# A two-layer convolution and attention kernel: fixed places for every operation, variance from sums made together, one PReLU term added by GpSimd, five product buffers

## The chip, the cores and the metric

The kernel runs on one core of a Trainium2 chip. The metric is the device time of one execution in microseconds (us), lower is better. Engines are called as the profile calls them: PE (TensorE, matmuls; PEld its weight loads), DVE (VectorE), ACT (ScalarE), POOL (GpSimd), SP (SyncE, which issues every DMA here). Each engine works through its own list of instructions in order; waits between engines are semaphores.

## What is computed

The input x is 16 images of 256 channels of 56 x 56 values in float32. Two residual layers follow each other; `_gn` is a group norm with 32 groups and no affine part.

```python
# layer 0
xq = sign(_gn(x) + bias)
out = 0
for i, d in enumerate((1, 3, 5)):                 # three dilations
    y = conv3x3(xq, binary_weight(w[i]), dilation=d, groups=4)
    y = y + cb[i] - move1[i]
    y = where(y >= 0, y, alpha[i] * y)            # PReLU
    out = out + y + move2[i]
mean, var = out.mean(channels), out.var(channels)
x = x + (out - mean) * rsqrt(var + 1e-5) * gamma + beta
# layer 1
q, k, v = split(qkv_w @ _gn(x) + qkv_b)           # 8 heads of 8 channels each
k, v = unfold3x3(k) + dwconv(k) + ..., unfold3x3(v) + dwconv(v) + ...
attn = softmax((q * k).sum(channel), over the 9 neighbours)
x = x + proj_w @ (attn * v).sum(neighbours) + proj_b
```

## The kernel before

Two half images lie one above the other on the 128 partitions (64 channels of a group each), so that a matmul works on quarters of the array. An image is cut into two *units* (u = 0, 1), each of 7 rows in each quarter of the image: a full-size operation covers 128 partitions x 784 values (2 x 392, two PSUM banks). PSUM is a ring of four such double banks (`banks`, kind "ps").

For an image b, the stages are:

- `stats`, `norm0`, `sign` (lines 420 to 457): load the four channel groups, sum and sum of squares on ACT with its accumulator (L424), the group norm's shift, the sign into a padded bf16 tile `sgn` (L449), then halo copies by DMA.
- `conv{u}` (lines 489 to 540): for each of 4 groups and 3 dilations, 36 matmuls of `sgn` and `wconv` into one double bank (L499). The PReLU of it is written as alpha times the value plus (1 - alpha) times Relu. Into the tile `ct` go: for the first dilation a scaled copy on ACT (L518), for the other two a multiply-add on DVE that reads PSUM and `ct` (L525); then Relu in place on ACT (L531), and for all three a second multiply-add on DVE (L537), after which the bank is free.
- `mean{u}`, `var{u}`, `root{u}`, `scale{u}` (lines 576 to 654): the layer norm over channels. All four `ct` are summed over channels by PE (L548), ACT copies the sum (L588), PE spreads it to all partitions (L566), DVE subtracts it from each `ct` (L595; `mv2`, the constant part of the PReLUs, is added here too), ACT squares (L602), PE sums the squares into a bank of its own. Small operations on ACT and DVE (L612 to L617) make the inverse root with one Newton step, PE spreads it, DVE multiplies (L624), POOL adds the result to the residual `xt` (L638), ACT takes the squares for the next group norm (L645).
- `fold` (lines 657 to 721): the second group norm is folded into the QKV weights `wf` (POOL, L667) and a bias.
- `qkv{u}` (lines 723 to 765): 48 matmuls per unit (L729), evicted by ACT into `qt`, `kt`, `vt`.
- `prod{u}`, `term{u}`, `soft{u}` (lines 776 to 844): for each of 9 neighbours a product of q and the shifted k, `p` (L785, three buffers), which PE sums into scores of four heads (L807; the bias term, first, waits for the first three products); a 32 x 32 transpose, the softmax on DVE, ACT and POOL, and a transpose back into `at`.
- `value{u}`, `proj{u}` (lines 846 to 926): for each of 10 terms PE spreads the weights (L857), DVE multiplies by the shifted v (L869), and the terms are summed into the first one (L883); PE projects (L903), DVE adds to `xt` (L914), and the unit is stored by four DMAs (L924).

All operations are first recorded in a `Plan` and then issued in an order that the plan makes (lines 113 to 232). Each recorded operation has its engine, a planned cost and a priority: twice the image number plus a number that `ORDER` gives for its stage and its index in the stage. `Plan.emit` keeps a planned clock for every engine and every buffer, and takes again and again the ready operation that can start first, with the priority as the second key, so that the order of the engines' lists comes from planned costs. `either` (lines 357 to 361) records an operation that POOL or DVE may do: POOL, unless DVE would be done earlier by the margin `LEAN` (by `LAST` in the last image). By the trace this put all adds L638, all products L785 but 12 of the last image, and all value adds L883 but 5 of the last image on POOL. The lists of the engines repeat from image to image in the middle of the program, and mix the convolutions of one image with the attention of the image before it.

Of the kernel before, what the change touches and what calls it, by code (L numbers as in the profile page):

```python
# [2 lines left out]

# [11 lines left out]
P = 128  # L15
# [4 lines left out]
PADC = 5  # L20
# [25 lines left out]


# [11 lines left out]
class Buf:  # L59


    def __init__(self, kind):
        self.kind, self.left, self.tile, self.end = kind, 0, None, 0.0
# [5 lines left out]
class Op:  # L69
    def __init__(self, engines, prio, emit, bufs, port, late):  # L70
        self.engines, self.prio, self.emit = engines, prio, emit
        self.bufs, self.port, self.late = bufs, port, late
        self.after, self.wait, self.ready = [], 0, 0.0

ORDER = {
    "first": (-3.81,),
    "second": (88.59,),
    "start": (-2.38, 18.89, -7.71, 3.29),  # L80
    "weights": (-4.65, -9.01, 0.64, 24.68, 23.33, 21),
    "stats": (10.49, 30.86, 22.58, 94.91),
    "norm0": (32.82,),
    "sign": (19.48, 99.46, -6.27, -5.4),
    "conv0": (-1.69, 4.96, 26.11, 0.66, 0.85, 19.36, -4.07, -1.86, 4.93, -11.22, -8.26, 19.59),
    "conv1": (-5.78, -8.78, 98.87, 0.22, 0.26, 6.89, -8.83, 30.63, 33.62, 1.84, 19.38, 25.39),
    "load0": (90.92,),
    "load1": (8.24,),
    "mean0": (-9.77,),
    "mean1": (20.13,),  # L90
    "var0": (-12.01, -8.88, 19.47, -0.22),
    "var1": (-14.66, 26.56, 89.22, -12.67),
    "root0": (23.78,),
    "root1": (-9.89,),
    "scale0": (100.7, 21.53, 3.58, 99.01),
    "scale1": (-10.73, -4.27, -0.4, 21.4),
    "fold": (-8.77,),
    "qkv0": (-0.15, -11.55, 19.01),
    "qkv1": (10.85, 1.84, 96.23),
    "prod0": (28.81, -0.84, -7.11, -6.13, -10.3, 7.62, -0.09, -4.95, 20.71),  # L100
    "prod1": (27.44, 23.38, -3.2, 99.25, 31.01, -10.92, -1.88, -1.61, -3.25),
    "term0": (19.37, 27.66, 25.15, 17.81, -9.38, 9.45, -1.68, 20.87, -1.36, 21.48),
    "term1": (24.14, 22.52, 28.6, 3.33, 8.91, 2.55, 1.92, 35.5, 4.7, 21.73),
    "soft0": (-4.91,),
    "soft1": (7.25,),
    "value0": (8.34, -0.46, -5.88, 1.95, 0.4, 8.91, 0.58, 26.08, -5.98, 34.72),
# [6 lines left out]
class Plan:  # L113

    HOP = 0.1
    LEAN = 26.94
    LAST = -11.31
    AHEAD = 0.13

# [41 lines left out]
    def emit(self):  # L167
# [4 lines left out]
        while ready:  # L172
            short, best = set(), {}
            for x in ready:
# [15 lines left out]
                if held:  # L190
                    continue
# [1041 lines left out]
```

## Time and profile before

| | us |
|---|---|
| median of three runs | 2156.07 |
| lowest, highest | 2154.64, 2160.12 |
| the profiled execution, as timed | 2157.43 |
| its span, first to last instruction | 2154.9 |
| DVE L537, second multiply-add, x384, mean of one | 1.027 |
| DVE L525, multiply-add of two dilations, x256, mean of one | 1.024 |
| ACT L518, scaled copy of the first dilation, x128, mean of one | 0.910 |
| DVE L595, subtraction of the mean, x128, mean of one | 1.023 |
| DVE L869, product with v, x288, mean of one | 0.969 |
| POOL L785, products, x276, mean of one | 1.726 |
| POOL L883, value adds, x251, mean of one | 1.906 |
| POOL L638, residual adds, x128, mean of one | 1.860 |
| mean granted clock of PE, as a share | 0.948 |

The profile gives for each group of instructions their busy time and what ended the idle time of the engine before them. The busy shares are means over the whole span; what a change in one stage is worth is read from windows of that stage and from the timeline, where an idle time of an engine stands in brackets together with the instruction that ended it. Neighbouring instructions on DVE overlap a little, so that their distance from start to start is somewhat less than the duration of one.

### The profile page before, as it was taken

What the parts mean: (1) busy time and instruction counts of PE and PEld (TensorE: products, weight loads), DVE (VectorE), ACT (ScalarE), POOL (GpSimd) and SP (SyncE); (2) the same over time, 40 slices, a digit from 0 to 9 for tenths busy, and PEclk for the clock granted to TensorE, in tenths of its full rate; (3) what the DMA queues carried; (4) which work ended last, traced back from release to release, by engine and by line L of the source; (5) the groups of instructions that cost most, each with busy time, mean ns of one, the idle gap of its engine ahead of it and who ended that gap; (6) DMA issues with size and microseconds to landing.
All of it is one profiled execution on the core that took longest, in us unless ns stands there. A gap on an engine that the chain in (4) does not pass through costs nothing.

```text
span 2154.9 us, 70853 instructions
## 1 busy us (share of the span) xinstructions
PE 1823.2 (85%) x31770; PEld 889.5 (41%) x31770; DVE 1697.7 (79%) x2327; ACT 1189.6 (55%) x1581; POOL 1276.5 (59%) x762
## 2 busy tenths in 40 slices
PE   6679898888989889898988989898898989879684
PEld 5444353434435343443534344353434435434231
DVE  7676969789696977969698796968879696986856
ACT  8675556565565756556575655647565565533220
POOL 2116657585675748557574865747486574746743
PEclk9889999999999999999999999999999999989896
DMA  8742534644453454445445444644444454041212
GB/s 208 165 92 67 123 79 111 130 95 91 110 130 83 111 121 97 93 104 133 91 111 117 100 94 95 138 94 111 108 102 101 95 133 100 7 100 23 61 31 60
DMA packets 102416, 216.26 MB, mean 100 GB/s; under 512 B 10720, under 2 KB 84832, under 8 KB 102112
## 3 DMA queue, kind: packets, MB, share of 16 engines
q1 hardware_dynamic: 102112, 211.74, 44.5%
q8 instruction: 248, 4.06, 0.8%
q14 instruction: 56, 0.46, 0.1%
HBM read 154.91 MB, written 51.38 MB: 96 GB/s over the span
## 4 chain that ended last, share of the span: by engine, by line
PE 42%; DVE 32%; POOL 10%; ACT 7%; issue 7%; DMA 2%; SPq 0%; POOLq 0%; DVEq 0%; ACTq 0%
PE banks L499 13%; PE banks L729 10%; PE banks L807 8%; POOL m L883 6%; DVE m L869 6%; DVE ct L537 6%; PE banks L857 5%; DVE ct L525 5%; DVE xt L914 4%; ACT banks L531 3%; DVE ct L595 3%; POOL xt L638 2%; PE banks L566 2%; PE banks L903 2%; DVE et L821 1%
## 5 line engine op out<-in xcount | busy, mean ns | idle before, releaser
L499 PE MATMUL banks<-sgn,wconv 64*64 64x392 bf16 x13824 | 680.2, 340 | 78.9 <-DVE m L869 32.1
L785 POOL TENSOR_TENSOR p<-qt,kt 128x784 f32<-128x784 f32 x276 | 467.0, 1726 | 326.2 <-ACT kt L762 179.3
L883 POOL TENSOR_TENSOR m<-m 128x784 f32<-128x784 f32 x251 | 478.3, 1906 | 248.1 <-DVE m L869 232.8
L499 PEld LDWEIGHTS <-wconv 64*64 64x64 bf16 x13824 | 438.6, 107 | 373.4 <-issue 217.4
L531 ACT ACTIVATE banks<-banks,cbi,csc 128x784 f32<-128x784 f32 x384 | 370.2, 973 | 203.2 <-DVE ct L525 192.4
L537 DVE SCALAR_TENSOR_TENSOR ct<-banks,oalpha,ct 128x784 f32<-128x784 f32 x384 | 389.4, 1027 | 98.4 <-ACT banks L531 89.3
L525 DVE SCALAR_TENSOR_TENSOR ct<-banks,asc,ct 128x784 f32<-128x784 f32 x256 | 262.0, 1024 | 186.9 <-PE banks L499 180.7
L857 PE MATMUL banks<-at,wv 64*32 64x392 f32 x5120 | 300.0, 533 | 61.3 <-DVE m L869 44.2
L638 POOL TENSOR_TENSOR xt<-xt,ct 128x784 f32<-128x784 f32 x128 | 237.2, 1860 | 190.4 <-DVE ct L624 189.6
L869 DVE TENSOR_TENSOR m<-banks,vt 128x784 f32<-128x784 f32 x288 | 278.2, 969 | 54.8 <-PE banks L857 48.7
L807 PE MATMUL banks<-p,wk 32*64 32x392 f32 x4608 | 245.4, 517 | 38.6 <-POOL p L785 38.2
L729 PE MATMUL banks<-xt,wf 64*64 64x392 f32 x3072 | 269.0, 496 | 2.8 <-POOL wf L667 2.8
L424 ACT ACTIVATE junk<-xh 128x1568 bf16<-128x1568 f32 x128 | 193.2, 1509 | 103.2 <-DMA xh<-in_x 101.4
L645 ACT ACTIVATE junk<-xt,pr 128x784 bf16<-128x784 f32 x128 | 121.2, 947 | 106.4 <-POOL xt L638 105.2
L602 ACT ACTIVATE sq<-ct 128x784 f32<-128x784 f32 x128 | 109.4, 857 | 125.2 <-DVE ct L595 102.5
L518 ACT ACTIVATE ct<-banks,asc 128x784 f32<-128x784 f32 x128 | 116.4, 910 | 98.8 <-PE banks L499 87.5
L729 PEld LDWEIGHTS banks<-xt,wf 64*64 64x64 f32 x3072 | 116.0, 134 | 129.2 <-issue 104.4
L857 PEld LDWEIGHTS banks<-at,wv 64*32 64x32 f32 x5120 | 63.3, 108 | 220.6 <-DVE m L869 110.9
L807 PEld LDWEIGHTS banks<-p,wk 32*64 32x64 f32 x4608 | 80.3, 133 | 161.1 <-POOL p L785 83.0
L903 PE MATMUL banks<-m,wp 64*64 64x392 f32 x1024 | 122.3, 584 | 26.1 <-DVE m L891 21.8
L595 DVE SCALAR_TENSOR_TENSOR ct<-ct,mv,banks 128x784 f32<-128x784 f32 x128 | 125.4, 1023 | 17.4 <-PE banks L566 17.4
L914 DVE SCALAR_TENSOR_TENSOR xt<-banks,prb,xt 128x784 f32<-128x784 f32 x128 | 128.1, 1028 | 10.4 <-PE banks L903 9.7
(102 smaller groups left out, 1518.8 us busy)
## 6 DMA issues: line engine op xcount, KB each, us to landing
xh<-in_x SPq DMA_DIRECT2D x248, 392.0 KB, 5.6
xt<-in_x SPq DMA_DIRECT2D x128, 392.0 KB, 7.1
out<-xt SPq DMA_DIRECT2D x128, 392.0 KB, 5.8
sgn<-sgn SPq DMA_DIRECT2D x128, 41.2 KB, 4.7
p<-in_w SPq DMA_DIRECT2D x12, 144.0 KB, 5.9
wq<-in_wqkv SPq DMA_DIRECT2D x1, 384.0 KB, 6.1
cst<-in_consts SPq DMA_DIRECT2D x1, 336.0 KB, 2.9
wk<-in_wk_a SPq DMA_DIRECT2D x1, 320.0 KB, 5.8
```

The costliest lines, as they stand in the source:

```text
L499: nc.tensor.matmul(out=ps[q * GC : (q + 1) * GC, h, 0:SN], lhsT=wconv[h * GC : (h + 1) * GC, g, d, tap, :], rhs=sgn[g][h * GC : (h + 1) * ...
L525: lambda: nc.vector.scalar_tensor_tensor(ct.tile, n(), asc[:, g, s], ct.tile, ALU.mult, ALU.add),
L531: lambda: nc.scalar.activation(n(), n(), AF.Relu, bias=cbi[:, g, s], scale=csc[:, g, s]),
L537: lambda: nc.vector.scalar_tensor_tensor(ct.tile, n(), oalpha[:, g, s], ct.tile, ALU.mult, ALU.add),
L638: lambda e, g=g: e.tensor_tensor(xt[:, g], xt[:, g], ct[g].tile, ALU.add),
L729: nc.tensor.matmul(out=ps[h * D : (h + 1) * D, q, 0:SN], lhsT=wf[q * GC : (q + 1) * GC, g, j, :], rhs=xt[q * GC : (q + 1) * GC, g, h, :], ...
L785: e.tensor_tensor(p.tile.rearrange("p x (r w) -> p x r w", w=W), _view(qt[:, 0, u * SN :], [(NU * SN + LANES, 2), (W, SR), (1, W)]), shift ...
L807: nc.tensor.matmul(out=ps[rt // 2][q * 64 : (q + 1) * 64, rt % 2, 0:n], lhsT=wk[r, j, :], rhs=rhs, start=s == 0, stop=s == 9,)
L857: nc.tensor.matmul(out=ps[rt * 32 : (rt + 1) * 32, q, 0:SN], lhsT=wv[q * 64 : (q + 1) * 64, j, :], rhs=at[q * 64 : (q + 1) * 64, rt, 0:SN] ...
L869: lambda j=j, m=m, ps=ps: nc.vector.tensor_tensor(m.tile.rearrange("p x (r w) -> p x r w", w=W), _view(ps[:, 0, :], [(512, 2), (W, SR), (1 ...
L883: lambda e, m=m, acc=acc: e.tensor_tensor(acc.tile, acc.tile, m.tile, ALU.add),
L914: lambda g=g, ps=ps: nc.vector.scalar_tensor_tensor(xt[:, g], ps[:, :, 0:SN], prb[:, g : g + 1], xt[:, g], ALU.add, ALU.add),
```

## The change

It has six parts.

1. `Plan` has no planned clock any more. Every single operation, not only every stage, has a place in `ORDER`: a number per operation in the order in which a stage records them, for the first image (names with ^), the last (with $) and all between. The place is this number plus 126.77 times the image's number. `emit` sorts by place and takes each time the first operation in that list whose inputs are recorded and for whose buffers there is room.
2. Which of the `either` operations DVE does is written down in `ON_VECTOR`. Over the program DVE has 90 of 288 products, 42 of 256 value adds, 5 of 128 residual adds and 20 of the 128 new adds of part 4.
3. The variance is taken as the mean of squares less the square of the mean. As each `ct` is done, ACT squares it and PE adds both `ct` and its square to two halves of one double bank. The mean's subtraction comes later and no longer stands between. `mv2` goes into the first dilation's ACT operation as its bias.
4. For the third dilation (`POOLED`), the scaled copy is made by ACT into a new tile `rl` (one buffer) instead of the multiply-add by DVE; the second multiply-add goes into `rl`; and an `either` operation adds `rl` to `ct`.
5. `p` has five buffers instead of three (the bias term still waits for the first three products).
6. Small ones: the scratch tile `junk` is gone (ACT's squares write over their inputs or over `ct`), the four row sums of x of the first image are made by DVE, and an identity matrix that nothing read is no longer loaded.

```diff
 class Plan:
...
+    def at(self, stage, b):
+
+        self.stage = stage + ("^" if b == 0 else "$" if b == self.last else "")
+        self.image = b
...
+        if engines:
+            emit = partial(emit, engines[k in ON_VECTOR.get(self.stage, ())])
...
+        o = Op(PERIOD * self.image + ORDER[self.stage][k], emit, bufs)
...
+        self.free = {k: n for k, (_, n) in self.kinds.items()}
+        todo = sorted(self.ops, key=lambda o: o.place)
+        while todo:
+            o = next((o for o in todo if not o.wait and self.room(o)), None)
...
-    kind("p", UNIT, 3)
+    kind("rl", UNIT, 1)
+    kind("p", UNIT, 5)
...
+        to = Buf("rl") if d in POOLED else ct
         if d == 0:
             act(
-                lambda: nc.scalar.mul(ct.tile, n(), asc[:, g, s]),
-                [ps, ("scales", g, d)],
+                lambda: nc.scalar.activation(
+                    ct.tile, n(), AF.Identity, bias=mv2[:, g : g + 1], scale=asc[:, g, s]
+                ),
+                [ps, ("scales", g, d), "mv2"],
                 [ct],
             )
+        elif d in POOLED:
+            act(lambda: nc.scalar.mul(to.tile, n(), asc[:, g, s]), [ps, ("scales", g, d)], [to])
         else:
...
         dve(
-            lambda: nc.vector.scalar_tensor_tensor(ct.tile, n(), oalpha[:, g, s], ct.tile, ALU.mult, ALU.add),
+            lambda: nc.vector.scalar_tensor_tensor(to.tile, n(), oalpha[:, g, s], to.tile, ALU.mult, ALU.add),
             [ps],
-            [ct],
+            [to],
         )
+        if d in POOLED:
+            either(
+                lambda e: e.tensor_tensor(ct.tile, ct.tile, to.tile, ALU.add),
+                [to],
+                [ct])
...
     def channel_norm(b, u, ct, xt, sums):
 
         ps = Buf("ps")
+        for g in range(NG):
+            plan.at(f"var{u}", b)
+            sq = Buf("sq")
+            act(lambda g=g, sq=sq: nc.scalar.activation(sq.tile, ct[g].tile, AF.Square), [ct[g]], [sq])
+
+            def sum_of_both(g=g, sq=sq):
+                lanes_sum(ps, 0, ct[g], g)
+                lanes_sum(ps, 1, sq, g)
+
+            pe(sum_of_both, [ct[g], sq], [ps])
+        plan.at(f"root{u}", b)
+        ms, t, v, r, s = (Buf("lv") for _ in range(5))
+        mean, square = (lambda i=i: ps[:, i, 0:VB] for i in range(2))
...
+        act(lambda: nc.scalar.copy(ms.tile, mean()), [ps], [ms])
+        dve(lambda: tt(t.tile, mean(), ms.tile, ALU.mult), [ps, ms], [t])
+        dve(lambda: stt(v.tile, t.tile, -1.0, square(), ALU.mult, ALU.add), [ps, t], [v])
+        dve(lambda: nc.vector.tensor_scalar(v.tile, v.tile, 0.0, EPS_LN, ALU.max, ALU.add), [], [v])
...
+        mb = Buf("ps")
+        lanes_spread(mb, ms)
         for g in range(NG):
             dve(
-                lambda g=g: nc.vector.scalar_tensor_tensor(
-                    ct[g].tile, ct[g].tile, mv2[:, g : g + 1], mb[:, :, 0:SN], ALU.add, ALU.subtract
-                ),
+                lambda g=g: nc.vector.tensor_tensor(ct[g].tile, ct[g].tile, mb[:, :, 0:SN], ALU.subtract),
                 [mb],
                 [ct[g]],
             )
```

The places are 1,233 numbers. Two stages of an image between the first and the last, and what DVE takes over there:

```python
PERIOD = 126.77
...
    "prod0": (116.53, 111.63, 76.46, 123.95, 83.34, 111.84, 101.11, 109.04, 89.08),
    "term0": (171.06, 171.22, 171.24, 169.25, 173.12, 132.34, 175.86, 176.35, -53, 106.25),
...
    "conv1": (25,),
    "prod0": (1, 2, 3, 5, 6),
    "value0": (7, 10),
```

## The prediction

> **What bounds the kernel now.** I read the busy shares first, then the shares of the chain of waits, then the times of the output stores (they give the period of one image), then busy time in stretches of one period, and last the timeline of PE and of DVE in that period.
>
> ```profile
> PE 1823.2 (85%) x31770; PEld 889.5 (41%) x31770; DVE 1697.7 (79%) x2327; ACT 1189.6 (55%) x1581; POOL 1276.5 (59%) x762
> ...
> PE 42%; DVE 32%; POOL 10%; ACT 7%; issue 7%; DMA 2%; SPq 0%; POOLq 0%; DVEq 0%; ACTq 0%
> ```
>
> No engine is full, and the chain changes between PE and DVE. The stores of each image's first unit show a steady state (here images 6 and 7):
>
> ```profile
> 1008.14 4.77 SPq L924 DMA_DIRECT2D out<-xt  x4
> 1134.37 4.77 SPq L924 DMA_DIRECT2D out<-xt  x4
> ```
>
> The period is 126.2 us. From the first such store (249.1) to image 14's (2022.7) are 14 periods of 126.7 us on average; 249.1 us lie before them and 132.2 us after. The same period in three stretches (columns: stretch, length, busy us of PE, weight loads, DVE, ACT, POOL, then clock, DMA share, GB/s):
>
> ```profile
> 1008.00:1046.40 38.40, 32.08 (x584) 17.92 (x577) 36.20 (x63) 19.70 (x31) 23.37 (x16) 0.96 0.49 105
> 1046.40:1094.20 47.80, 44.37 (x752) 20.80 (x748) 30.30 (x39) 25.95 (x33) 28.77 (x18) 1.00 0.42 93
> 1094.20:1134.40 40.20, 34.85 (x649) 15.16 (x649) 36.44 (x39) 28.11 (x36) 28.87 (x16) 0.96 0.55 124
> ```
>
> This table carries the prediction. In the middle stretch (call it A: fold, QKV, scores) PE is busy 44.4 of 47.8 us and DVE has 17 us to spare. In the other two (B: values, projection, most convolutions) DVE is busy 72.6 of 78.6 us and PE waits. So a period is PE's work in A plus DVE's work in B, 44.4 + 72.6 = 117.0 us, plus 9.4 us of losses: 3.4 in A, 6.0 in B. PE's stalls, by what ended them:
>
> ```profile
> 1013.82 0.54 PE L548 MATMUL banks<-sq,cst 128*32 128x196 f32 x8 [1.66 <-ACT sq L602]
> ...
> 1027.48 1.58 PE L566 MATMUL banks<-lv,cst 64*64 64x196 f32 x16 [2.11 <-DVE lv L617]
> ...
> 1094.24 0.92 PE L807 MATMUL banks<-p,wk 32*64 32x392 f32 x16 [2.50 <-POOL p L785]
> ...
> 1110.47 1.74 PE L499 MATMUL banks<-sgn,wconv 64*64 64x392 bf16 x36 [1.20 <-DVE m L869]
> ```
>
> The first two belong to the variance, but DVE is full there, so the queue behind it is the cause. The third is the products: POOL, with three buffers, is late at the end of A. DVE's spare time, and its pace where it is full:
>
> ```profile
> 1010.03 1.02 DVE L525 SCALAR_TENSOR_TENSOR ct<-banks,asc,ct 128x784 f32<-128x784 f32 x1
> 1010.97 0.96 DVE L869 TENSOR_TENSOR m<-banks,vt 128x784 f32<-128x784 f32 x1
> 1011.85 1.96 DVE L595 SCALAR_TENSOR_TENSOR ct<-ct,mv,banks 128x784 f32<-128x784 f32 x2
> ...
> 1057.76 1.03 DVE L525 SCALAR_TENSOR_TENSOR ct<-banks,asc,ct 128x784 f32<-128x784 f32 x1 [6.06 <-PE banks L499]
> ...
> 1065.57 1.03 DVE L525 SCALAR_TENSOR_TENSOR ct<-banks,asc,ct 128x784 f32<-128x784 f32 x1 [4.24 <-PE banks L499]
> ```
>
> From start to start, a full-size scalar_tensor_tensor costs 0.95 us of DVE and a tensor_tensor 0.89 us; these are my DVE prices.
>
> **What the Trainium skill says.** "SBUF — State Buffer", section "Who interferes with whom": a VectorE instruction with two SBUF inputs and a GpSimd instruction that reads SBUF exclude each other for the whole of the one that started first. The trace agrees, both ways (the POOL lines are two adds each, the last line is DVE's usual 1.12 us subtraction):
>
> ```profile
> 1010.19 3.80 POOL L883 TENSOR_TENSOR m<-m 128x784 f32<-128x784 f32 x2 [1.09 <-DVE m L869]
> ...
> 1108.25 1.12 DVE L833 TENSOR_TENSOR et<-et,mx 128x936 f32<-128x936 f32 x1
> ...
> 1108.47 4.56 POOL L883 TENSOR_TENSOR m<-m 128x784 f32<-128x784 f32 x2 [1.13 <-DVE m L869]
> ...
> 2104.38 2.00 DVE L833 TENSOR_TENSOR et<-et,mx 128x936 f32<-128x936 f32 x1
> ```
>
> "Perfetto Trace Analysis", section "Identifying the Most-Contended Engine", warns that matmul busy time does not measure the distance to the roofline. I therefore use PE's 44.4 us only as what this same matmul list takes when nothing else holds it (93% of A), not as a floor of the hardware.
>
> **The change part by part**, per interior image. Counts are read from the two built programs' instruction orders; both repeat exactly from image to image in the middle.
>
> *Third dilation.* DVE loses 8 of 16 multiply-adds (L525): 8 x 0.95 = 7.6 us. ACT gains 8 scaled copies at 0.91 (row L518): 7.3 us on 74 of 126, hidden. POOL gains 7 adds at 1.86 = 13.0 us, DVE one (0.9).
>
> *Products and value adds.* Before, all 18 products and 16 adds of an interior image are on POOL. After, DVE has 5 products (4.5 us) and 2 adds (1.8 us). POOL loses 5 x 1.69 + 2 x 1.86 = 12.2 us, so POOL stays at about 82 us. The 5 products stand in A, in DVE's spare 17 us. With DVE taking them the first unit's nine cost at most 5 x 0.9 + 4 x 1.69 = 11.3 us even if they exclude each other wholly, against 15.2. With that, and five buffers, I take the 2.5 us stall as gone.
>
> *Variance.* Sum and sum of squares now run on the uncentred ct as each group ends, so the squares no longer wait for the mean's spread and DVE's subtraction. The matmul list is the same in number and shape. The subtraction becomes a tensor_tensor (-0.06 us x 8); the small DVE work is six operations for four, two more per unit at about 0.4 (rows L614 to L617): +1.6 us in all, half of it in B. mv2 moves into the first ACT operation as a bias: nothing.
>
> *Order.* On PE, A holds 3 convolutions instead of 5 and 17 score steps instead of 18, all else equal: 2 x 1.67 + 0.84 = 4.2 us of PE leave A for B, where PE has slack (67 + 4 of 78). On DVE, B then holds 22 final multiply-adds instead of 20 (+1.9), 6 of the others instead of 11 (-4.75), the 2 value adds and one conv add (+2.7), two small operations (+0.8) and the cheaper subtraction (-0.2): +0.45 us. So A's PE work is 40.2, B's DVE work 73.1, the sum 113.3 instead of 117.0.
>
> *Losses.* A's 3.4 us are 2.5 of products, 0.9 of mean spreads waiting for DVE: I take 1.0 (0 to 3.4). B's 6.0 us are waits of DVE for PE where the stretches meet and single ones between; nothing in the change removes them as such: I take 6.0 (3 to 10). New: three two-input DVE operations in B beside POOL adds. Each loses nothing or up to the 1.86 us of the POOL operation ahead, 0 to 5.6 us; the one measured collision of DVE cost 0.88 and not all meet: I take 0.7. Period: 113.3 + 1.0 + 6.0 + 0.7 = 121.0, that is 5.4 less than 126.4.
>
> *Edits at nothing.* ACT's squares write into xh and ct instead of a bf16 scratch; ACT's 50 idle us cover any difference. It holds ct (7 buffers) about 1 us longer; if ct were short, that would cost up to 1 us a unit. The SP list is the same 656 transfers. The constant tile lacks 64 KB, at the start, hidden.
>
> *Ends.* Head: four row sums of x go from ACT (1.5 + 0.19 each) to DVE, and DVE sheds the third dilation. ACT is the fullest in the first 134 us (107 busy, DVE 95) and gets about as much as it gives: -3 us (-10 to +6). Tail: after the last transpose the trace has 41 us, with 22 us of DVE work and waits for POOL's adds in the one chain that sums the values. After the change most of the adds are DVE's own (7 for 5, 24.5 us of work) and fewer waits for POOL at 1.86 remain: -6 us (-12 to 0).
>
> *Sum.* 14 x 5.4 = 75.6; with 6 and 3, 84.6. The profiled execution took 2157.4 us (span 2154.9 and 2.5 around it), 1.4 over the median of 2156.1: 2157.4 - 84.6 - 1.4 = 2071.4, so 2071 us.
>
> **Rivals.**
> 1. *Losses go too* (chance 0.13). If the fixed order also takes half of B's losses and all of A's, the period is 113.3 + 3 = 116.3: 14 x 10.1 = 141 less, with -12 at the ends 2003 us. For it: 6.0 us of losses are there to be had. Against: PE would be 95% busy (111 of 116), and PE and DVE still wait for each other through four PSUM buffers.
> 2. *Exclusion eats it* (0.15). If the two-input DVE operations in B lose a full 1.86 us each and B's losses rise to 7, as the POOL adds they hold up arrive late: 113.3 + 1 + 7 + 5.6 = 126.9 less overlap of some 2.5 = 124.4: 2 x 14 = 28 and 6 at the ends, 2122 us. For it: both collisions shown above. Against: only 3 of 8 lie in B.
> 3. *Slower: the one rl buffer* (0.10). The third dilation's scaled copy on ACT needs rl, freed only when POOL's add has read it; that add stands in POOL's order behind value adds waiting for DVE. Behind the copy on ACT's in-order queue stand the next Relu operations, and behind these DVE, PSUM and PE. Least life of rl is 0.91 + 0.97 + 1.03 + 1.86 = 4.8 us, and one comes every 15 us, so up to 10 us of queueing are free. POOL's longest stretch without such an add (4 folds, 11 products, softmax and some adds) is 34 us; ACT's order has no such copy in most of it, but two near its end. If each of the 8 waits more than 0.75 us on the path (6 us), the gain is gone; at 1.2 us the period is 130.6: +4.2 x 14 - 9, or 2206 us.
>
> **How the numbers follow.** Forecast 0.62, rivals 0.13, 0.15, 0.10. The low end is the first rival's less its best part (period 117: 2012); the high end holds most of the second (2132). About 0.3% (6 us) is what a measurement can tell from none. The forecast and rivals 1 and 2 are faster (0.88, leaving 0.02 for none); slower 0.10.
>
> **What would show it.** Right: stores of first units 120 to 122 us apart; DVE's gaps of 6 and 4 us in A filled by products; no wait of PE for products over 1 us; POOL near 82 us a period. Wrong: ACT idle before the rl copies, ended by POOL (rival 3); DVE products or adds at 1.5 us or more (rival 2); PE over 94% busy (rival 1). If A and B overlap differently in the new order, the sum of PE in A and DVE in B is the step that fails.

## The result, and the profile after

The changed kernel takes 2190.5 us (median; 2186.1 to 2193.4), the kernel before 2158.1 us beside it: the ratio is 1.0149, with a 95% interval of 1.0124 to 1.0174. It is slower by 32 us, where 2071 us, a gain of about 85 us, were forecast.

First come two lines from the page of the profiled execution (2191.91 us, span 2190.1): busy time by engine, and the chain of waits by engine.

```profile
PE 1821.6 (83%) x31770; PEld 935.9 (43%) x31770; DVE 1848.9 (84%) x2406; ACT 1278.9 (58%) x1701; POOL 1295.1 (59%) x750
...
PE 52%; DVE 31%; ACT 8%; issue 5%; DMA 2%; POOL 1%; SPq 0%; DVEq 0%; POOLq 0%; ACTq 0%
```

PE's and POOL's busy times are nearly those of before. DVE is busy 151 us longer, although the change takes about as much work from it as it gives. So instructions of DVE have become longer; the groups below show which. The chain's POOL share has gone from 10% to 1%, and PE's from 42% to 52%.

The stores of the first unit (images 6 and 7, the timeline of SP's queue):

```profile
1033.79 4.80 SPq L1046 DMA_DIRECT2D out<-xt  x4
...
1163.46 2.82 SPq L1046 DMA_DIRECT2D out<-xt  x3
```

The period shown is 129.7 us. From the first such store (263.9 us) to image 14's (2057.3) are 14 periods of 128.1 us on average, where the kernel before had 126.7 and the forecast 121.0. Against before that is +19.8 us for the periods, +14.8 before the first store and +0.6 after the last: together the 35.2 us by which the spans differ.

The same period in the prediction's stretches (columns as there). The middle one is A, from the sums of the fold to the seventeenth score step; the other two are B.

```profile
1033.80:1076.80 43.00, 37.65 (x734) 22.37 (x734) 39.93 (x57) 27.12 (x38) 29.66 (x19) 0.96 0.65 141
1076.80:1118.96 42.16, 40.87 (x680) 19.97 (x676) 34.02 (x43) 20.16 (x27) 22.75 (x13) 1.00 0.36 75
1118.96:1163.46 44.50, 34.53 (x566) 14.77 (x559) 37.52 (x45) 32.39 (x43) 31.10 (x17) 0.85 0.41 95
```

A takes 42.2 us with PE busy 40.9; 41.2 and 40.2 were forecast. B takes 87.5 us where 79.8 were forecast. DVE is busy 77.45 us in B (forecast 73.1 and 0.7 of exclusion), and for 10.05 us of B it is not (forecast 6.0). The clock column shows a second thing: 0.85 in the last stretch, where the kernel before had 0.96.

The groups of instructions (operation | busy us, mean ns of one | idle us before them and what ended it). The rows of the second block are from the kernel before:

```profile
L645 PE MATMUL banks<-sgn,wconv 64*64 64x392 bf16 x13824 | 708.3, 352 | 109.3 <-DVE m L996 86.4 <-DVE rl L684 7.3 <-DVE xt L1036 3.4
...
L936 PE MATMUL banks<-p,wk 32*64 32x392 f32 x4608 | 233.6, 497 | 1.4 <-DVE p L914 1.1 <-issue 0.2
...
L914 DVE TENSOR_TENSOR p<-qt,kt 128x784 f32<-128x784 f32 x90 | 131.0, 1504 | 75.4 <-ACT kt L892 57.2 <-PE banks L936 13.2 <-ACT kt L879 4.9
L671 ACT ACTIVATE rl<-banks,asc 128x784 f32<-128x784 f32 x128 | 116.4, 909 | 120.6 <-PE banks L645 107.6 <-DVE ct L690 7.8 <-POOL ct L690 5.1
L1009 DVE TENSOR_TENSOR m<-m 128x784 f32<-128x784 f32 x42 | 65.3, 1554 | 2.3 <-POOL m L1009 0.5
L961 DVE TENSOR_TENSOR et<-et,mx 128x936 f32<-128x936 f32 x32 | 54.6, 1707 | 0.1
L743 DVE TENSOR_SCALAR lv<-lv 128x196 f32<-128x196 f32 x32 | 32.7, 1022 | 0.6
```

```profile
L499 PE MATMUL banks<-sgn,wconv 64*64 64x392 bf16 x13824 | 680.2, 340 | 78.9 <-DVE m L869 32.1
...
L833 DVE TENSOR_TENSOR et<-et,mx 128x936 f32<-128x936 f32 x32 | 38.4, 1200 | 0.0
```

DVE's products (L914) and value adds (L1009), which read two SBUF tiles, take 1.50 and 1.55 us. A product that reads one tile and PSUM (L996) takes 0.97. The softmax's subtraction (L961), 1.20 us in the kernel before, now takes 1.71. The wait of PE for products (L936) is gone: 1.4 us in the whole run. But the convolutions (L645) wait 86.4 us for DVE's product `m` (32.1 us before, L499), because in this program PE may not write a bank before DVE has read it.

The timeline shows where that happens. Here is the same stretch on all three engines. First DVE:

```profile
1128.45 0.96 DVE L996 TENSOR_TENSOR m<-banks,vt 128x784 f32<-128x784 f32 x1
1129.52 2.32 DVE L1009 TENSOR_TENSOR m<-m 128x784 f32<-128x784 f32 x1
1131.76 2.77 DVE L961 TENSOR_TENSOR et<-et,mx 128x936 f32<-128x936 f32 x1
1134.45 1.84 DVE L996 TENSOR_TENSOR m<-banks,vt 128x784 f32<-128x784 f32 x2
1136.21 0.96 DVE L1009 TENSOR_TENSOR m<-m 128x784 f32<-128x784 f32 x1
1137.09 1.02 DVE L684 SCALAR_TENSOR_TENSOR ct<-banks,oalpha,ct 128x784 f32<-128x784 f32 x1
```

POOL at that time:

```profile
1129.15 1.86 POOL L690 TENSOR_TENSOR ct<-ct,rl 128x784 f32<-128x784 f32 x1
1130.95 2.58 POOL L777 TENSOR_TENSOR xt<-xt,ct 128x784 f32<-128x784 f32 x1
```

And PE, with the idle time before each in brackets:

```profile
1129.46 0.89 PE L985 MATMUL banks<-at,wv 64*32 64x392 f32 x16 [0.41 <-DVE m L996]
1135.46 3.15 PE L645 MATMUL banks<-sgn,wconv 64*64 64x392 bf16 x36 [5.10 <-DVE m L996]
```

DVE's add at 1129.52 meets POOL's add of 1129.15 and ends only after it (2.32 us). POOL's next add then meets the rest of DVE's and takes 2.58 instead of 1.86, and the softmax's subtraction behind it takes 2.77 instead of 1.12. The two products that free PE's banks stand behind these in DVE's list, and so PE stands still for 5.10 us. When it goes on, 36 matmuls take 3.15 us; in the kernel before such 36 took 1.74. This knot is no single event: in thirteen periods PE stands still here for 5.08 to 5.28 us, and the matmuls after it are slow every time. Not all of these 5.1 us come from the collision; an experiment below shows how much of the stall is left without it.

A second collision lies in the first stretch. There the root's multiplication, two small SBUF tiles, takes 1.90 us beside a POOL add; in the other unit, in A, the same one takes 0.36:

```profile
1050.60 1.90 DVE L747 TENSOR_TENSOR lv<-lv 128x196 f32<-128x196 f32 x1
```

```profile
1050.43 1.84 POOL L1009 TENSOR_TENSOR m<-m 128x784 f32<-128x784 f32 x1 [0.62 <-DVE m L996]
```

The add (1.4 us over its usual time), the subtraction (1.6) and this multiplication (1.5) together make about the 4.35 us by which DVE's busy time in B is above 73.1.

### The profile page after: what moved, and what is told of

The parts are those of the page before. It is cut to its first block, busy times and chain, and to the rows that moved or that the text cites. A ratio compares the mean times of both kernels' runs of the same rounds, so it can differ in the third digit from the quotient of the medians.

```text
span 2190.1 us, 71001 instructions
## 1 busy us (share of the span) xinstructions
PE 1821.6 (83%) x31770; PEld 935.9 (43%) x31770; DVE 1848.9 (84%) x2406; ACT 1278.9 (58%) x1701; POOL 1295.1 (59%) x750
## 4 chain that ended last, share of the span: by engine, by line
PE 52%; DVE 31%; ACT 8%; issue 5%; DMA 2%; POOL 1%; SPq 0%; DVEq 0%; POOLq 0%; ACTq 0%
PE banks L645 22%; PE banks L861 9%; PE banks L936 7%; PE banks L985 6%; DVE m L996 4%; PE banks L698 4%; DVE xt L1036 4%; DVE et L949 3%; DVE ct L754 3%; ACT xh L571 2%; DVE ct L684 2%; DVE m L1009 2%; ACT banks L679 2%; PE banks L712 2%; DVE ct L674 2%
## 5 line engine op out<-in xcount | busy, mean ns | idle before, releaser
L645 PE MATMUL banks<-sgn,wconv 64*64 64x392 bf16 x13824 | 708.3, 352 | 109.3 <-DVE m L996 86.4
L645 PEld LDWEIGHTS <-wconv 64*64 64x64 bf16 x13824 | 463.0, 111 | 399.9 <-issue 250.0
L914 POOL TENSOR_TENSOR p<-qt,kt 128x784 f32<-128x784 f32 x198 | 366.9, 1879 | 327.4 <-ACT kt L892 161.4
L1009 POOL TENSOR_TENSOR m<-m 128x784 f32<-128x784 f32 x214 | 399.9, 1869 | 252.9 <-DVE m L996 188.5
L690 POOL TENSOR_TENSOR ct<-ct,rl 128x784 f32<-128x784 f32 x108 | 200.8, 1859 | 224.4 <-DVE rl L684 154.1
L996 DVE TENSOR_TENSOR m<-banks,vt 128x784 f32<-128x784 f32 x288 | 275.2, 965 | 53.9 <-PE banks L985 51.8
L684 DVE SCALAR_TENSOR_TENSOR ct<-banks,oalpha,ct 128x784 f32<-128x784 f32 x256 | 260.3, 1022 | 47.3 <-ACT banks L679 43.1
L936 PE MATMUL banks<-p,wk 32*64 32x392 f32 x4608 | 233.6, 497 | 1.4 <-DVE p L914 1.1
L914 DVE TENSOR_TENSOR p<-qt,kt 128x784 f32<-128x784 f32 x90 | 131.0, 1504 | 75.4 <-ACT kt L892 57.2
L571 ACT ACTIVATE xh<-xh 128x1568 f32<-128x1568 f32 x120 | 180.8, 1507 | 10.4 <-DMA xh<-in_x 8.2
L671 ACT ACTIVATE rl<-banks,asc 128x784 f32<-128x784 f32 x128 | 116.4, 909 | 120.6 <-PE banks L645 107.6
L664 ACT ACTIVATE ct<-banks,mv,asc 128x784 f32<-128x784 f32 x128 | 128.3, 1003 | 54.7 <-PE banks L645 54.3
L595 ACT ACTIVATE sgn<-xh,g 128x1568 bf16<-128x1568 f32 x64 | 105.5, 1652 | 74.8 <-PE banks L645 70.0
L684 DVE SCALAR_TENSOR_TENSOR rl<-banks,oalpha,rl 128x784 f32<-128x784 f32 x128 | 130.4, 1019 | 20.1 <-ACT banks L679 16.9
L674 DVE SCALAR_TENSOR_TENSOR ct<-banks,asc,ct 128x784 f32<-128x784 f32 x128 | 130.1, 1024 | 16.0 <-PE banks L645 15.9
L781 ACT ACTIVATE ct<-xt,pr 128x784 f32<-128x784 f32 x128 | 120.3, 941 | 38.8 <-POOL xt L777 38.4
## 6 DMA issues: line engine op xcount, KB each, us to landing
sgn<-sgn SPq DMA_DIRECT2D x128, 41.2 KB, 4.3
```

What stands on the lines that cost most here:

```text
L571: lambda func=func, col=col: nc.scalar.activation(inside(g) if b == 0 else image(xh), image(xh), func, accum_out=sums[:, col : col + 1]),
L645: nc.tensor.matmul(out=ps[q * GC : (q + 1) * GC, h, 0:SN], lhsT=wconv[h * GC : (h + 1) * GC, g, d, tap, :], rhs=sgn[g][h * GC : (h + 1) * ...
L684: lambda: nc.vector.scalar_tensor_tensor(to.tile, n(), oalpha[:, g, s], to.tile, ALU.mult, ALU.add),
L690: lambda e: e.tensor_tensor(ct.tile, ct.tile, to.tile, ALU.add),
L914: e.tensor_tensor(p.tile.rearrange("p x (r w) -> p x r w", w=W), _view(qt[:, 0, u * SN :], [(NU * SN + LANES, 2), (W, SR), (1, W)]), shift ...
L936: nc.tensor.matmul(out=ps[rt // 2][q * 64 : (q + 1) * 64, rt % 2, 0:n], lhsT=wk[r, j, :], rhs=rhs, start=s == 0, stop=s == 9,)
```

## The experiments

Theory: the operations with two SBUF inputs that the change gives to DVE and POOL's operations exclude each other, and what is queued behind them (softmax, products that free PSUM) makes PE stall. Rivals: the fixed order costs the time, whatever the operands are; the new variance does; the head does. Line numbers of the runs differ by a few from those of the changed kernel. All ratios are to the kernel before, with 95% intervals in brackets.

### Back to POOL: three adds, or five products (adds, prods)

```diff
 ON_VECTOR = {
...
-    "conv1": (25,),
...
-    "value0": (7, 10),
```

> The changed kernel, but in the images between the first and the last the two value adds and the one convolution add that DVE does go back to POOL; the order of the operations stays. Theory (exclusion: DVE operations with two SBUF inputs and POOL operations block each other, in the stretch where DVE is full): the add of 2.32 us and the like go, the period falls from 128.1 by 2 to 4 us, about 2145 to 2165 us in all, DVE busy falls by some 60 us. Rival (the fixed order itself costs the time; DVE has room for these adds): POOL's longer chain of adds makes the values later, 2190 to 2215 us.

Measured: 2149.3 us, ratio to before 0.9963 (0.9949 to 0.9978). The subtraction is back at 1.196 us, and the mean period is 125.15 us in the profiled execution, the fastest of twelve. Three adds decide whether the change is slower or faster. This version beats the changed kernel by 41 us and the kernel before by 0.4%.

```diff
-    "prod0": (1, 2, 3, 5, 6),
```

> The changed kernel, but in the images between the first and the last all products are POOL's. Theory (exclusion hurts where DVE is full, and DVE is not full in the score stretch): the products on DVE take 1.5 instead of 0.97 us there, but in time that DVE had to spare; nine products on POOL take 4 us longer than shared ones, so 2185 to 2215 us. Rival (every DVE operation with two SBUF inputs costs time wherever it stands): 2150 to 2175 us.

Measured: 2255.0 us, 1.0445 (1.042 to 1.047), slower still than the theory expected. The five products are worth 65 us on DVE although each takes 1.5 us there. PE still does not wait for the products themselves (2.3 us in the run), but its wait for DVE's `ct` before the first score steps of a unit goes from 8.4 to 40.2 us; how POOL's longer list leads to that was not followed. So exclusion alone does not condemn a two-input operation on DVE.

### Which of the three adds (adds_a, adds_y)

In adds_a only the two value adds go to POOL (`"value0"` removed), in adds_y only the conv add (`"conv1"` removed).

> The changed kernel, but of DVE's adds in the middle images only the two value adds go back to POOL; the one convolution add stays on DVE. The trace has the value add at 2.32 us beside POOL, the softmax subtraction behind it at 2.77, then a PE stall of 5.1 us and half-speed matmuls after it; the convolution add stands at 0.97. Theory (this one knot is what the run with all three moved has gained): 2145 to 2160 us. Rival (any DVE operation less helps alike, so two thirds of the gain): 2160 to 2170 us.

> The counterpart: only the one convolution add of the middle images goes back to POOL. Theory (the knot at the value adds): no gain, 2183 to 2195 us. Rival (any DVE operation less helps): 2170 to 2180 us.

Measured: 2151.7 us, 0.998 (0.9971 to 0.9989), and 2195.3 us, 1.0177 (1.0161 to 1.0192). So it is the two value adds. DVE's timeline of adds_a at the same place:

```profile
1110.14 0.96 DVE L995 TENSOR_TENSOR m<-banks,vt 128x784 f32<-128x784 f32 x1
1111.02 1.12 DVE L960 TENSOR_TENSOR et<-et,mx 128x936 f32<-128x936 f32 x1
1112.06 0.97 DVE L995 TENSOR_TENSOR m<-banks,vt 128x784 f32<-128x784 f32 x1
1113.89 0.97 DVE L995 TENSOR_TENSOR m<-banks,vt 128x784 f32<-128x784 f32 x1 [0.86 <-POOL m L1008]
```

From one product to the next are 1.9 us instead of 6.0 (1128.45 to 1134.45 above), and PE's wait for them is 1.03 us. A wait of DVE for POOL of 0.86 us is the price.

### Exclusion or work: the same places, one input less (onein_adds, onein_prods, onein_both)

Moving the adds takes two things from DVE: exclusion, and 1.9 us of its own work a period. These runs keep the number of DVE's operations and their order, and take the second SBUF input away. The Trainium skill ("SBUF — State Buffer", section "Who interferes with whom") says that a reduction never contends with GpSimd on this chip. So a reduction over an axis of length 1 stands in for the add or the product; the kernel then leaves these terms out of its sums. The two edits, in part:

```diff
-                        lambda e, m=m, acc=acc: e.tensor_tensor(acc.tile, acc.tile, m.tile, ALU.add),
...
+                        if one and e is nc.vector:
+                            e.tensor_reduce(acc.tile, m.tile.unsqueeze(3), AX.X, ALU.add)
...
```
```diff
             def product(e, j=j, p=p):
+                if u == 0 and 0 < b < NB - 1 and e is nc.vector:
+                    q = _view(qt[:, 0, u * SN :], [(NU * SN + LANES, 2), (1, SN), (1, 1)])
+                    e.tensor_reduce(p.tile, q, AX.X, ALU.add)
+                    return
```

> The changed kernel with its places; in images 1 to 14 each of the two value adds of DVE (terms 7 and 10 of the first unit) is a reduction over an axis of length 1: it reads m only, one SBUF input, and writes 784 values to the sum's tile, so these terms and those before them are left out of the sum. DVE's own time for it should stay near 0.95 us, its waits for other engines are the same, only the exclusion with POOL can go. Theory A (exclusion is what the two adds cost): as good as the kernel with both adds on POOL, 2145 to 2165 us, L1009-like reductions near 0.95 us instead of 1.55, softmax subtraction near 1.2 us. Theory B (two more operations in a queue that is full in this stretch, whatever they read, and their waits): stays at 2180 to 2192 us, of which 14 x 2 x 0.9 = 25 us is DVE time.

> The changed kernel; in images 1 to 14 each of the five products of DVE is a reduction over an axis of length 1 that reads q only (one SBUF input) and writes 784 values to p, so k is left out of these products. Theory A (exclusion in the score stretch costs what the trace shows, 1.50 instead of 0.97 us for each of the five): up to 70 x 0.53 = 37 us less, 2150 to 2175. Theory B (PE is the limit there and the late products are covered by five buffers): 2183 to 2195, unchanged although the products fall to 0.95 us.

> Both of these at once: in images 1 to 14 the two value adds and the five products of DVE each read one SBUF input; those terms are left out as said there. Nearly no exclusion is left but the conv add, the softmax subtraction and the small operations of the variance. If exclusion is the whole miss of the prediction (119 us less 18 at the head and 7 at the tail): 2085 to 2110 us, period near 122. If it is a part only: 2125 to 2160, and the sum of stretches missed something else as well.

Measured: 2161.5 us, 1.0023 (0.9999 to 1.0047), with runs from 2149.8 to 2170.0; 2179.4 us, 1.0107 (1.0085 to 1.0129); 2154.4 us, 0.9984 (0.9971 to 0.9998). Groups of DVE in onein_both:

```profile
L916 DVE TENSOR_REDUCE p<-qt 128x784 f32<-128x784 f32 x70 | 64.0, 964 | 47.2 <-ACT qt L879 26.9 <-PE banks L940 20.3
L965 DVE TENSOR_TENSOR et<-et,mx 128x936 f32<-128x936 f32 x32 | 51.7, 1614 | 0.1
L1014 DVE TENSOR_REDUCE m<-m 128x784 f32<-128x784 f32 x28 | 26.9, 961 | 1.4
```

The reductions take 0.96 us beside a POOL with nearly the same work: the page's statement holds here. The subtraction still collides (mean 1.61, where 1.2 was expected), as do the small operations. The DVE timeline of this run at the same place, and below it PE's:

```profile
1110.41 0.96 DVE L1000 TENSOR_TENSOR m<-banks,vt 128x784 f32<-128x784 f32 x1
1111.48 0.97 DVE L1014 TENSOR_REDUCE m<-m 128x784 f32<-128x784 f32 x1
1112.37 1.59 DVE L965 TENSOR_TENSOR et<-et,mx 128x936 f32<-128x936 f32 x1
1113.88 1.84 DVE L1000 TENSOR_TENSOR m<-banks,vt 128x784 f32<-128x784 f32 x2
```

```profile
1114.90 1.74 PE L645 MATMUL banks<-sgn,wconv 64*64 64x392 bf16 x36 [2.57 <-DVE m L1000]
```

Here the products are 3.5 us apart instead of 6.0, PE's stall is 2.57 us instead of 5.10, and the 36 matmuls after it take 1.74 instead of 3.15 us. So the collision of the add, 1.4 us, had cost PE 2.5 us of standstill at this place; the rest of the stall is left. That holds for nine of thirteen periods (2.56 to 2.60 us). In the other four the stall is 4.4 us: there the subtraction takes 3.4 us, since it waits for two POOL adds in a row. So these runs do not take all exclusion away, and what they price is a lower bound of it.

The value adds' second input is worth 29 us (2190.5 to 2161.5), the products' 11, both together 36, of which the 14 periods hold 31 (128.1 to 125.9 on average). In the products alone DVE saves 45 us (90 at 1.504 us in the changed kernel, against 70 at 0.964 and 20 at 1.135 in onein_prods), and a quarter of that reaches the end, which fits A waiting for PE. A product without k also does not wait for `kt` any more (57.2 us of idle in the row L914 above), so the 11 us are not exclusion alone. For the value adds the trace shows no such second change: DVE's idle time before them is 2.3 us in the run, as in the changed kernel.

Without this exclusion the change takes as long as the kernel before, and its period is shorter (125.9 for 126.7); the head, 11 us longer in this profile than before, eats that gain. So this exclusion is what makes the period longer than before. It is not all that the forecast missed: the period is 125.9 us on average, not 121.0. One period of this run (125.15 us, columns as above):

```profile
1016.80:1059.19 42.39, 36.60 (x734) 22.25 (x734) 39.86 (x57) 27.20 (x38) 29.66 (x19) 1.00 0.66 143
1059.19:1100.92 41.73, 40.87 (x680) 19.98 (x676) 30.56 (x43) 20.17 (x27) 20.80 (x13) 1.00 0.36 75
1100.92:1141.95 41.03, 33.34 (x566) 14.66 (x559) 34.92 (x45) 32.22 (x43) 31.30 (x17) 0.88 0.44 104
```

A is 41.7 us, nearly the forecast. B is 83.4: DVE is busy for 74.8 us, and for 8.6 us it is not. That remainder was 6.0 in the kernel before, and it grows even without the exclusion of the adds and products.

### The variance (var, adds_v)

The tensor_scalar L743 and the multiplication L747 of the root read only SBUF and take 1.02 and 1.03 us in the mean; operations of that size with an input from PSUM take 0.36. In var the variance before the root and the Newton step's product lie in free columns of the sums' double bank; in adds_v (the three adds on POOL) only the first of these does. The edit of adds_v:

```diff
-        dve(lambda: stt(v.tile, t.tile, -1.0, square(), ALU.mult, ALU.add), [ps, t], [v])
-        dve(lambda: nc.vector.tensor_scalar(v.tile, v.tile, 0.0, EPS_LN, ALU.max, ALU.add), [], [v])
+        dve(lambda: stt(square(), t.tile, -1.0, square(), ALU.mult, ALU.add), [t], [ps])
+        dve(lambda: nc.vector.tensor_scalar(v.tile, square(), 0.0, EPS_LN, ALU.max, ALU.add), [ps], [v])
```

> The changed kernel, but the six small DVE operations of the inverse root keep v and s in the free columns of the double bank of the sums, so that none has two SBUF inputs and none copies SBUF to SBUF. Theory (exclusion): each of them takes 0.35 to 0.4 us again (from means of about 1.0), PE's wait of 3.0 us for the inverse root shrinks to about 1.5, the period falls by 1.5 to 3 us, 2150 to 2170 us in all. Rival (the double bank is held some microseconds longer, and banks are short): no gain or a loss, 2188 to 2205 us.

> All three adds on POOL, and the variance before its epsilon is kept in the double bank of the sums, so that the tensor_scalar reads PSUM and cannot be shut out by POOL; the bank is held for one small operation more, not for the whole root. Theory (exclusion): that operation falls from 1.03 to about 0.36 us, ACT's 95 us of waiting for it shrink, 2130 to 2146 us. Rival (banks are so short that any longer hold costs more): 2160 us or more.

Measured: 2235.6 us, 1.0356 (1.0333 to 1.0379), and 2189.8 us, 1.0154 (1.0136 to 1.0172), the latter 41 us over adds. The operations that were moved did fall to 0.36 us, but the double bank is freed later, and PE waits for it. In adds_v, PE's timeline:

```profile
1104.22 3.15 PE L643 MATMUL banks<-sgn,wconv 64*64 64x392 bf16 x36 [2.28 <-DVE lv L741]
```

One of four double banks, held for one or two small operations more, costs more here than their exclusion. So these runs do not price the small operations' exclusion, and they say nothing about the new variance itself, which no run took out of the new order.

### What the third dilation is worth (adds_nopool)

With the adds on POOL, the third dilation goes back to DVE: no `rl`, no copy on ACT, no add on POOL; the places of what remains are kept.

```diff
-        to = Buf("rl") if d in POOLED else ct
+        to = ct
...
-        elif d in POOLED:
-            act(lambda: nc.scalar.mul(to.tile, n(), asc[:, g, s]), [ps, ("scales", g, d)], [to])
```

> All three adds on POOL, and the third dilation's first multiply-add is again DVE's into ct, in the place of ACT's copy; rl and its adds on POOL are left out. DVE has 131 us more to do. Theory (DVE is what the value stretch waits for, and taking this work off it is the gain in the change): 5 to 7 us more a period, 2215 to 2250 us. Rival (the gain is in the order alone, this part does nothing): 2140 to 2165 us.

Measured: 2412.0 us, 1.1183 (1.1166 to 1.12), 263 us over adds and far outside both expectations. The 128 multiply-adds come to 122 us of DVE at 0.95. That the rest comes from a list whose places were made for other operations was not tested, so this run does not price the third dilation.

### The parts alone in the order of before (g_p4, g_var, g_rl, g_all)

The kernel before with its own planner and one part each: a fourth buffer for `p` (with five, its planner finds no order), the new variance with the sums made when all four `ct` are there, the third dilation through `rl`, and all operations of the change at once.

```diff
-    kind("p", UNIT, 3)
+    kind("p", UNIT, 4)
```
```diff
+        to = Buf("rl") if d == 2 else ct
+        if d == 2:
+            act(0.92, lambda: nc.scalar.mul(to.tile, n(), asc[:, g, s]), [ps, ("scales", g, d)], [to])
...
```

> The kernel before with its planner, and one thing changed: four product buffers instead of three (with five the planner finds no order). Theory (the product buffers are late at the end of the score stretch, 2.5 us of PE a period): 2120 to 2145 us. Rival (the time goes elsewhere, as DVE is what the value stretch waits for): 2145 to 2165 us.

> The kernel before with its planner, and one thing changed: the variance from sums of ct and of its squares made together (here when all four ct are there), mv2 in the first ACT operation, the subtraction a tensor_tensor. Theory (the operations themselves are no loss; the planner keeps small two-input operations of DVE apart from POOL's): 2130 to 2165 us. Rival (the new variance is itself the loss, whatever the order): 2175 us or more.

> The kernel before with its planner, and one thing changed: the third dilation's scaled copy on ACT into rl (one buffer), its add on POOL. DVE has 131 us less to do, POOL 238 us more. Theory (DVE is what the value stretch waits for): period down by 3 to 6 us, 2070 to 2115 us. Rival (the one rl buffer and POOL's longer list hold ACT up, and so PE): 2160 us or more.

> The kernel before with its planner, and all the changes of operations at once: rl, the variance, five product buffers. Only the fixed places and the split of POOL's work with DVE are missing. Theory (the operations gain, and the fixed order with DVE operations against POOL loses it again): 2060 to 2140 us. Rival (the operations lose by themselves): 2180 us or more.

Measured: 2570.5 (1.1908; 1.1886 to 1.193), 2481.3 (1.151; 1.1487 to 1.1533), 2675.9 (1.2396; 1.2375 to 1.2418) and 2556.3 us (1.1848; 1.1831 to 1.1866). All four are hundreds of microseconds above what the theories expected, and these runs can't price the parts. The old planner's order with its priorities fits the unchanged operations only: even one buffer more costs 19%. With nearly the same operations as the changed kernel (g_all) it is 366 us slower than the fixed places. So the parts can be told apart only inside the new order.

### The head (head, adds_h, adds_h2)

In head the first image's row sums go back to ACT; in adds_h and adds_h2 (adds on POOL) the second image's statistics go behind the first image's last sign, in adds_h with their loads, in adds_h2 without. The edits of head and of adds_h2, in part:

```diff
-            if b == 0 and key == "sums":
-                dve(
...
```
```diff
+        place = PERIOD * self.image + ORDER[self.stage][k]
+        if self.image == 1 and self.stage == "stats" and k % 3:
+            place = max(place, 48.0 + 2.5 * k)
```

> The changed kernel, but the four row sums of x of the first image are made by ACT again. Theory A (the head is 15 us longer because DVE's first small operations were blocked 7 us by POOL's fills of the constant tiles, and by the order of loads): 2183 to 2190 us, the first store still near 260 us. Theory B (the four reductions of 1.8 us on DVE stand ahead of the weights and delay the first convolutions): the first store at 252 us or earlier, 2175 to 2180 us.

> The kernel with the three adds back on POOL (2149 us), and in the head the second image's loads and statistics (12 operations) placed behind the first image's last sign instead of ahead of it, spread over the first convolutions. Theory A (the fixed places let the next image's 8 statistics passes, 13 us of ACT, go ahead of the first image's last signs, and that is the head's remaining 9.5 us): first store at 249 to 254 us instead of 258.6, total 2139 to 2145. Theory B (the head is set by the weights' sums on DVE and the loads): first store 257 to 262, total unchanged at 2146 to 2153.

> The kernel with the three adds back on POOL (2149 us), and in the head only the second image's 8 statistics passes on ACT placed behind the first image's last sign; its loads keep their places. The run that moved the loads too was slower because ACT, in order, stood at passes whose data had been asked for late, with the evictions of the convolutions behind them (PE idle 21.7 us before L646, ended by a DVE multiply-add). Theory A (the passes ahead of the last sign are the head's remaining 9.5 us): no such idle, first store at 249 to 255 us, total 2139 to 2146. Theory B (the weights' sums and the loads set the head, the passes only fill ACT's waits): first store 256 to 262, total 2146 to 2153.

Measured: 2196.4 us (1.0176; 1.0156 to 1.0197), 2183.3 us (1.0122; 1.0103 to 1.0141), 2162.8 us (1.003; 1.0018 to 1.0042), with first stores at 264.2, 290.9 and 271.5 us (changed kernel 263.9, adds 258.6, before 249.1). None helped. In adds_h ACT, working in order, came to passes whose data had been asked for late, with the convolutions' evictions behind them:

```profile
58.82 0.89 ACT L672 ACTIVATE rl<-banks,asc 128x784 f32<-128x784 f32 x1
81.06 1.51 ACT L572 ACTIVATE xh<-xh 128x1568 f32<-128x1568 f32 x1 [21.35 <-DMA xh<-in_x]
```

In adds_h2 that stall is gone. ACT's timeline suggests why it still lost:

```profile
40.47 0.20 ACT L572 ACTIVATION_READ_ACCUMULATOR sgn<-xh 128x1 f32 x1
55.97 0.20 ACT L532 ACTIVATE g<-g 128x1 f32<-128x1 f32 x1 [15.30 <-DVE g L531]
```

In adds eight statistics passes stand in this time, in which ACT waits for DVE anyway. Behind the sign they share ACT with the convolutions' evictions.

One piece of the head is seen directly. DVE's timeline of the changed kernel (POOL fills seven tiles with zeros from 0.73 to 13.75 us):

```profile
3.58 7.14 DVE L1057 TENSOR_SCALAR oalpha<-pr 128x12 f32<-128x12 f32 x1
3.65 7.06 DVE L1058 TENSOR_TENSOR prb<-pr 128x4 f32<-128x4 f32 x1
```

In other profiles, with the same fills, the first one takes about 1.2 us. The profiles fall into two groups. In those of the changed kernel, adds_y, onein_adds and head it takes 6.8 to 7.1 us, and the first stores are at 263.9 to 266.8 us. In those of adds, adds_a, prods, onein_prods and onein_both it takes 1.2 to 1.3 us, and the first stores are at 258.6 to 261.6 us. Each kernel was profiled once, so whether this belongs to the kernel or to the execution is open.

## Why the prediction was wrong

*What bounds the kernel, and A.* The sum of PE in A and DVE in B held as a picture, and A came out as worked: PE 40.9 for 40.2, length 42.2 for 41.2. Products fill much of DVE's gaps there (the largest left in the period shown is 3.8 us, the wait for `kt`), PE's wait for products went from 2.5 us a period to 0.1, and POOL was busy 83.5 us in the period shown (82 forecast).

*The step that failed: the losses in B.* The prediction put the new ones as "0 to 5.6 us; the one measured collision of DVE cost 0.88 and not all meet: I take 0.7", and took B's old losses as unchanged, "I take 6.0". On the average of all periods the excess over 121.0 is 7.1 us. Taking one input from the two value adds removes 1.7 of them (126.4 in onein_adds), and from adds and products together 2.2, where 0.7 had been taken. Both are lower bounds of the exclusion. In the period shown the excess is 8.7 us: 1.0 in A, 3.65 in DVE's busy time in B, 4.05 in the time in which DVE is not busy there; in the period of onein_both it is 4.1.

Two things were left out of the term of 0.7. The first is the queue behind a collision. The value add that collides loses 1.4 us in most periods, within the range that was given. (In three of thirteen it loses 3.2, beyond it: it waits for two POOL adds in a row.) But the subtraction, which the change does not touch, collides in its turn, and the two products that PE needs come 2.5 us later, nearly twice the delay of the add itself. The second is the root's small operations. They were priced "at about 0.4", and two of the six took 1.02 and 1.03 us in the mean; in B the multiplication took 1.90 us in nearly every image. No term for PE's clock was in the sum at all.

*Rival 2 had the mechanism,* with DVE's products and adds at 1.5 us as its sign, but put it at 2122 us. It too bounded each loss by the POOL operation ahead, and let only 1 us a period follow from it.

*Rival 3 fell,* although its 2206 us came nearest. The copies into `rl` waited 5.1 us for POOL's adds and 7.8 us for DVE's in the whole run (the row L671 shows both), far from the 6 us a period that it needed. That the kernel is slower, as this rival said, is not its doing.

*B's remaining losses.* In the period of onein_both DVE is not busy for 8.6 us of B, where 6.0 were taken. The clock is 0.88 in its last stretch (0.96 in the kernel before), and DVE's waits for PE there are 5.1 us (2.6 before). That slow matmuls make DVE wait is argued from these numbers; no run kept PE's clock up, and so it is not shown. The Trainium skill ("TensorE: Matmul & The Clock Gate", section "HAM oscillation — how this bites in real kernels") warns of idle gaps of PE over about 3.4 us. The trace agrees for long gaps: the matmuls were slow after all thirteen stalls of 5.1 to 5.3 us in the changed kernel, and after all eight of 4.3 to 4.4 us in onein_adds and onein_both. But shorter gaps do not leave PE safe: after those of 2.55 to 2.60 us in these two runs, and of 2.28 us in adds_v, the same 36 matmuls took anything from 1.74 to 3.16 us. The mean clock over the run is 0.927 instead of 0.948.

*The head.* -3 was taken, +14.8 came. It rested on ACT being the fullest engine there, but in the new order ACT waits for DVE. About 5 us go with DVE's first operations behind the fills, by the two groups of profiles above; that was not tested by itself. The cause of the other 9 to 10 us was not found: three runs moved something in the head, and none shortened it. This stays open.

*The tail.* -6 was taken, +0.6 came. DVE has 14 products and 11 value adds of its last image there, all with two inputs from SBUF, but no run took these away. The tail is 127.9 us in adds, but 133.2 and 133.1 in adds_h and adds_h2 with the same adds on POOL, so single profiles of the same tail differ by 5 us, and the profile of adds can't be taken as a gain there. This is not settled either.

## What to carry to other kernels

When work moves to an engine that has to share with another, price the operation's own delay first, and then walk down its in-order list to the instruction that some third engine waits for: here 1.4 us on one add became 2.5 us more of standstill on PE. The same kind of operation can pay where nothing urgent stands behind it: five products at 1.5 us each were worth 65 us in the stretch where DVE had time. Look also for collisions of operations that the change does not move, and of small ones. An order made for a set of operations belongs to them, so undo one part inside the new order rather than try it alone in the old one.

## What the runs showed of the hardware that was not expected

- An exclusion can pass on: DVE's add delayed POOL's next one (2.58 instead of 1.86 us), and this one DVE's next operation (2.77 instead of 1.12).
- The operation that waits does not always get the next turn. In ten of the thirteen stalls of the changed kernel DVE's value add went in between POOL's two adds (2.3 us, and the subtraction after it 2.8); in the other three it took 4.1 us, and the subtraction 1.12.
- An f32 tensor_scalar with a single SBUF input took as long as two-input operations of its size did: a mean of 1.02 us for 196 values a row, from 0.26 to 1.93, and 0.36 with its input in PSUM. Single-input reductions of 784 values took 0.96 us throughout.
- Four operations on 4 to 12 values took until 10.7 us from 3.6, beside several of POOL's fills in a row; in other kernels' profiles, with the same fills, the first of them took about 1.2 us.
